# One rotation of PSUM banks, and small scalars moved off the vector engine, in a two-pass nucleus attention layer

## The chip, the cores and the metric

The kernel runs on one core of a Trainium2 chip. The metric is the device time of one execution in microseconds (us). The engines are TensorE (PE: matmuls and transposes, with its weight loads shown as PEld), VectorE (DVE), ScalarE (ACT), GpSimd (POOL) and SyncE (SP, which issues most transfers). Each takes its own instructions in order; semaphores tie them together.

## The reference

Two layers work on 4096 nodes of 256 features. Layer 0 is a graph attention with four heads over a 4096 x 4096 adjacency, plus a residual and a layer norm. Layer 1 does two steps. In each, every node gets a row of attention probabilities, cut to the smallest set whose mass reaches 0.9 (top-p), and its features are mixed with that row; a second stream is mixed by the normalised adjacency:

```
R = S + eye;  R = R / R.sum(-1)
for n in range(2):
    logits = (Xa @ W1.T @ W2.T) @ (Xa @ W3.T).T
    A = top_p(softmax(logits), 0.9);  A = A / A.sum(-1)
    Xf = R @ Xf
    Xa = A @ Xa
    Z = Z + Xf @ U1[n].T + Xa @ U2[n].T
out = layernorm(x + layernorm(x + Z) * g + b)
```

## The kernel before, in words

The first 950 us or so are layer 0 (`graph_attention`), which the change leaves alone. Layer 1 is `nucleus_layer`. It takes 32 tiles of 128 rows twice: a first pass (`place_first`, step 0) and a second one (`place_second`, step 1). A row tile of the class `RowTile` goes through these parts:

- the queries: a transpose of its features (L833, copied at L835), q1 (L918, copy L922), q (L926, copies L931 and L934);
- eight blocks of logits, 128 x 512 each, by `logits` (L950), copied from PSUM to SBUF by ACT in `logits_evict` (L961);
- the row maximum (`top`, L972; in the second pass over all 4096 columns), `spread` (L979) and `exp` (L990) on ACT, a handful of scalars;
- estimates of the threshold and moves towards it. In the second pass the estimates 1 and 2 use `estimate_half`: ACT runs over half of the row twice, once with Relu and once with Sign (L1064, L1067), and sums. `join` makes a mass of these sums (L1086, L1089 and L1096, on DVE) and takes its logarithm (L1079); `move` ends with the exponential L1134, which gives the new threshold t;
- `lift`, `final` (L1052 over 4096 columns, into w), then `tops` (32 maxima of eight, L965), `sort` (L1164, L1166), `edge` (L1173 to L1191, which ends with `fit`), `inside` and `cut` (L1224 on DVE, L1228 on POOL);
- the product with the features: eight blocks are transposed (L1240), copied to SBUF (L1249, or L1247 on DVE) and multiplied into `ap` (L1258), which is evicted at L1268.

Beside this a `Mix` multiplies a tile of the adjacency with the other stream (L1318, in two parts: a short and a long one), in eight chunks, into `rp`, copied at L1337 (`fx`). Each chunk's adjacency is loaded by SP. A finished mix of step 1 goes on to its output rows: four transposes (L833, copied at L835) and products (L1379) into `zp`; `out_sum` adds the residual `res` (L1405); `stats` takes mean and variance (L1390, L1392). `rsqrt_by_exp` gives the inverse deviation: logarithm and exponential on ACT (L64, L66), v, u and r1 on the engine that it is given (L68, L74, L75). `scale` makes `less` (L1400) and scales the row on ACT (L1401). This happens twice: `out_norm` (with gain and bias on POOL, L1411 to L1413) and, after `out_stats`, `out_store`, which also stores the row.

The order of work on PE, ACT, DVE and POOL is written out by hand. Every part is placed at a time in units of a tile, from the tables T1 and T2; `carry_out` sorts the parts by time and issues them, and each engine takes its share in that order. The order of SP's transfers is left to the scheduler of the framework.

[...] Here two (`ps_lg`) go to logits, three (`ps_tr`) to transposes, and three are single ones: `misc` (q1, q, zp), `ap` and `rp`. Each pool hands out its banks in turn.

Of the kernel before, what the change touches and what calls it, by code (L numbers as in the profile page):

```python
# [8 lines left out]
F32 = mybir.dt.float32  # L9
# [7 lines left out]
AF = mybir.ActivationFunctionType  # L17
# [5 lines left out]
P = 128  # L23
# [727 lines left out]
def nucleus_layer(  # L751
# [16 lines left out]
    ps_lg = ctx.enter_context(tc.tile_pool(name="f_lg", bufs=2, space=PSUM))  # L768
    ps_tr = ctx.enter_context(tc.tile_pool(name="f_tr", bufs=3, space=PSUM))
# [33 lines left out]
    shares = row("shares", SHARES)  # L803
    aims = [row(f"aims{n}", [aim for aim, _, _ in e]) for n, e in enumerate(EST)]
# [24 lines left out]
    def transposed(src, name, tag, bufs):  # L829

        tp = ps_tr.tile([P, 512], F32, tag="tr", name=f"tp_{name}")
        for c in range(2):
            nc.tensor.transpose(tp[:, c * P : (c + 1) * P], src[:, c * P : (c + 1) * P], ident)  # L833
        t = two.tile([P, 2, P], F32, tag=tag, name=f"t_{name}", bufs=bufs)
        nc.scalar.copy(t.rearrange("p c i -> p (c i)"), tp[:, : 2 * P])  # L835
        return t
# [38 lines left out]
    def keys(b):  # L875

        xt = []
        for c in range(2):
            tp = ps_tr.tile([P, 512], F32, tag="tr", name=f"tpk{b}_{c}")
            for q in range(4):  # L880
                nc.tensor.transpose(
                    tp[:, q * P : (q + 1) * P], xa[:, b * 4 + q, c * P : (c + 1) * P], ident
                )
            t = two.tile([P, 512], F32, tag="at", name=f"xkt{b}_{c}", bufs=3)
            if c:
                nc.scalar.copy(t, tp)
            else:
                nc.vector.tensor_copy(t, tp)
            xt.append(t)
        kp = ps_lg.tile([P, 512], F32, tag="lg", name=f"kp{b}")  # L890
# [8 lines left out]
    class RowTile:  # L899
# [12 lines left out]
        def front_transpose(self):  # L912
            self.xt = transposed(self.cur[:, self.i, :], f"x{self.id}", "xt", 3)

        def front_q1(self):
            qp = ps_one.tile([P, 512], F32, tag="misc", name=f"qp{self.id}")
            for c in range(2):
                nc.tensor.matmul(  # L918
                    qp[:DA, :P], w1[:, c, :], self.xt[:, c, :], start=c == 0, stop=c == 1
                )  # L920
            self.q1 = two.tile([DA, P], F32, tag="q1", name=f"q1_{self.id}", bufs=1)
            nc.scalar.copy(self.q1, qp[:DA, :P])  # L922

        def front_q(self):
# [3 lines left out]
            )  # L928
            self.q = two.tile([P, 2, P], F32R, tag="q", name=f"q_{self.id}")
            self.qp = qp[:, :P]  # L930
# [6 lines left out]
        def logits(self, pair):  # L937

            if pair == 0:
# [6 lines left out]
            self.lps[pair] = []  # L946
            for b in (2 * pair, 2 * pair + 1):
                lp = ps_lg.tile([P, 512], F32, tag="lg", name=f"lp{self.id}_{b}")
                for k in range(2):
                    nc.tensor.matmul(  # L950
                        lp,
                        self.q[:, k],
                        kT[:, b * 512 : (b + 1) * 512],
                        start=k == 0,
                        stop=k == 1,
                    )
                self.lps[pair].append((b, lp))

        def logits_evict(self, pair):
            for b, lp in self.lps.pop(pair):  # L960
                nc.scalar.copy(self.p[:, b * 512 : (b + 1) * 512], lp)  # L961

        def tops(self, src, b):
            for c in range(b * 4, (b + 1) * 4):
# [37 lines left out]
        def scalars(self):  # L1002
# [10 lines left out]
            self.aim = self.tiny("aim", len(self.est))  # L1013
# [3 lines left out]
        def scalars2(self):  # L1017
# [14 lines left out]
            else:  # L1032
                nc.vector.tensor_scalar(self.left, self.z, TOP_P - 1.0, None, ALU.mult)
                self.rest = small
                self.rzs = self.tiny("rzs", 2)
                nc.vector.tensor_scalar(self.rzs, shares, self.rz, None, ALU.mult)
# [45 lines left out]
        def join(self, k):  # L1082
            b, share = self.b, 0 if self.n and k == 0 else None
            if self.n and k:

                nc.vector.tensor_scalar(  # L1086
                    self.m, self.signs, self.t_half, self.t_all, ALU.mult, ALU.add
                )
                nc.vector.tensor_scalar(  # L1089
                    self.m, self.m, self.gaps, 0.0, ALU.subtract, ALU.max  # L1090
                )
# [4 lines left out]
                nc.vector.tensor_scalar(self.both, self.m, b, None, ALU.add)  # L1096
# [72 lines left out]
        def edge(self):  # L1169
# [13 lines left out]
            if self.n:  # L1183
# [6 lines left out]
                nc.vector.tensor_scalar(self.fit, out_of, -1.0, float(R), ALU.mult, ALU.add)  # L1190
                nc.vector.tensor_scalar(self.fit, self.fit, over, None, ALU.subtract)  # L1191
# [39 lines left out]
        def tops_of_pair(self, pair):  # L1231
            for b in (2 * pair, 2 * pair + 1):
                self.tops(self.p, b)

        def product_transpose(self, b):
            if b == 0:
                self.a_t = {}
            tp = ps_tr.tile([P, 512], F32, tag="tr", name=f"tpa{self.id}_{b}")
            for q in range(4):
# [4 lines left out]
                )  # L1244
            at = two.tile([P, 512], F32, tag="at", name=f"at{self.id}_{b}", bufs=3)
# [36 lines left out]
    class Mix:  # L1282
# [82 lines left out]
        def out_load_x(self):  # L1365
            rows = slice(self.i * P, (self.i + 1) * P)
            self.res = two.tile([P, D], F32, tag="res", name=f"res{self.id}", bufs=1)
            nc.sync.dma_start(self.res, x1_d[rows, :])

        def out_transpose(self, k):  # L1370
            src = xa[:, self.i, :D] if k == 2 else (self.xf1, self.fx[:, :D], None, self.xa2)[k]
            self.ot = transposed(src, f"o{k}{self.id}", "xt", 3)
# [14 lines left out]
        def stats(self, name):  # L1387
# [6 lines left out]
                nc, nc.vector, tiny, self.mv[:, 1:2], eps, f"{name}{self.id}"  # L1394
            )

        def scale(self):
            r = self.rstd()
            less = tiny.tile([P, 1], F32, tag="u", name=f"less{self.id}")
            nc.vector.tensor_scalar(less, self.mv[:, 0:1], r, -1.0, ALU.mult, ALU.mult)  # L1400
            nc.scalar.activation(self.h, self.h, AF.Identity, scale=r, bias=less)  # L1401

        def out_sum(self):
            self.h = two.tile([P, D], F32, tag="h", name=f"h{self.id}", bufs=1)
# [20 lines left out]
    def at(time, part, *args):  # L1425
# [7 lines left out]
        lag=0.218, out=0.344, qt=0.253, q1=0.460, q2=0.612, q3=0.680, space=0.125, apart=0.250, split=0.300,  # L1433
    )
    T2 = dict(top=0.468, spread0=0.650, spread1=0.516, exp0=0.655, exp1=0.607, scalars=0.731, scalars2=0.769, est0=0.808, join0=0.810, move0=0.828, join1=0.945, move1=1.088, est2=1.144, join2=1.232, move2=1.395, lift=1.491, final=1.649, tops=1.651, sort=1.842, edge=2.034, inside=2.135, cut=2.230, product=2.354, lag=0.090, out=0.060, qt=-0.086, q1=0.421, q2=0.453, q3=0.523, space=0.067, apart=0.074, mix=0.576, copy=0.042)
# [6 lines left out]
    def place_product(t, time, T):  # L1442
        space = T["space"]
        for k in range(8):
            at(time + k * space, t.product_transpose, k)
            at(min(time + k * space + T["lag"], time + 8 * space - 0.001), t.product, k)
# [3 lines left out]
    def place_queries(t, time, T):  # L1450
        at(time + T["qt"], t.front_transpose)
        at(time + T["q1"], t.front_q1)
        at(time + T["q2"], t.front_q)
        at(time + T["q3"], t.front_q_rest)

    def place_mix(m, time, length):

        for jc in range(8):
            at(time + (jc - 3.5) * length / 8, m.load, jc)
            at(time + jc * length / 8 + 0.03, m.mix, jc)  # L1460
# [4 lines left out]
    def place_first(t, time):  # L1465

        place_queries(t, time - 1, T1)
        for k in range(4):
            at(time + k * T1["apart"] + 0.01, t.logits, k)
            at(time + k * T1["apart"] + 0.01, t.logits_evict, k)  # L1470
            at(time + k * T1["apart"] + T1["tops"], t.tops_of_pair, k)
# [24 lines left out]
    def place_second(t, time):  # L1496

        place_queries(t, time - 1, T2)
        for k in range(4):
            at(time + k * T2["apart"] + 0.01, t.logits, k)  # L1500
            at(time + k * T2["apart"] + T2["copy"], t.logits_evict, k)
# [25 lines left out]
    def place_out(m, time):  # L1527
# [3 lines left out]
        for k in range(4):  # L1531
            at(time + 0.01 + 0.09 * k, m.out_transpose, k)
            at(time + 0.06 + 0.09 * k, m.out_product, k)
        at(time + 0.36, m.out_sum)
        at(time + 0.46, m.out_norm)
        at(time + 0.62, m.out_stats)
        at(time + 0.70, m.out_store)
# [457 lines left out]
```

## Time and profile before

| what | us |
|---|---|
| median of 3 runs (3446.21 to 3450.65) | 3448.2 |
| the profiled execution | 3446.17 |
| its span | 3444.2 |
| PE busy | 3120.7 |
| DVE busy | 2881.3 |
| ACT busy | 2528.7 |
| POOL busy | 611.2 |

The profile gives busy time by engine, in the whole span or in stretches of it; the granted clock of PE as a share of full speed; groups of instructions by line, with the mean time of one in ns; and waits, each put down to the instruction that ended it. Layer 0 takes up to about 950 us, the first pass from there to 1780, the second pass to 3380, and the last output rows run to the end. A wait on one engine costs nothing while another is the limit, so the stretches have to be read one by one.

### The profile page before, as it was taken

The page shows a single profiled execution, that of the slowest core. Times are in us where ns is not written, and L with a number is a line of the kernel's source. Part 1 is how long each engine was busy: PE and PEld are TensorE (multiplying, and loading weights), DVE is VectorE, ACT ScalarE, POOL GpSimd, SP SyncE. Part 2 cuts the span into 40 slices and gives each one's busy share as a digit, 9 for nine tenths or more (in the row PEclk, how much of TensorE's full clock was granted, in tenths as well). Part 3 has the DMA queues.
Part 4 walks back from the last instruction along what each step waited for, and adds up shares of the span by engine and source line. Part 5 has one row for each costly group of instructions (what it writes and reads, how often), then busy time and mean ns, then how long its engine had stood idle before and what let it go on. Part 6 is the DMA issues. An engine that isn't in the chain of part 4 may idle for free. (4 is left out here: it accounts for less than half of the span.)

```text
span 3444.2 us, 56052 instructions
## 1 busy us (share of the span) xinstructions
PE 3120.7 (91%) x19538; PEld 2162.0 (63%) x19538; DVE 2881.3 (84%) x8687; ACT 2528.7 (73%) x3978; POOL 611.2 (18%) x435
## 2 busy tenths in 40 slices
PE   8998888888889999999997898989899999999986
PEld 4422222222268888888875677777677777777775
DVE  4779989999848888888714999999999999899983
ACT  4678888888758888888725777777767667767752
POOL 1101450000000000000000222222222333343332
PEclk9999999999989999999998999999999999999998
DMA  9846453332152222322336444444644444444443
GB/s 214 138 114 138 131 131 113 114 111 86 62 167 95 96 105 107 108 95 95 103 100 172 116 116 126 119 118 126 169 111 113 109 112 110 110 111 116 112 104 78
DMA packets 637302, 402.60 MB, mean 117 GB/s; under 512 B 262672, under 2 KB 588304, under 8 KB 633936
## 3 DMA queue, kind: packets, MB, share of 16 engines
q1 hardware_dynamic: 626640, 315.03, 32.4%
q10 hardware_dynamic: 1536, 67.11, 5.4%
q0 software_dynamic: 8832, 16.78, 5.3%
q8 instruction: 155, 2.54, 0.3%
q14 instruction: 139, 1.14, 0.1%
HBM read 406.03 MB, written 118.62 MB: 152 GB/s over the span
## 5 line engine op out<-in xcount | busy, mean ns | idle before, releaser
L1318 PE MATMUL rp<-low,adj 128*128 128x258 f32 x1856 | 542.8, 382 | 26.7 <-ACT fx L1337 14.6
L1318 PE MATMUL rp<-p,short 128*128 128x256 f16 x1856 | 494.6, 293 | 2.2 <-DMA short<-adj_d 2.1
L1258 PE MATMUL ap<-xa,at 128*128 128x257 f32 x2048 | 490.9, 382 | 4.9 <-ACT at L1249 4.8
L617 DVE COPY_PREDICATED other<-mask,e 128x2048 f32<-128x2048 uint8 x176 | 454.0, 2594 | 49.3 <-ACT other L602 47.3
L1258 PE MATMUL ap<-xf,at 128*128 128x257 f32 x2048 | 483.5, 380 | 0.0
L950 PE MATMUL lp<-kT,q 128*128 128x512 f32 x1024 | 339.7, 458 | 106.0 <-ACT p L961 105.6
L595 ACT ACTIVATE e<-src,minus_flat,factors 128x2048 f32<-128x2048 f32 x176 | 367.9, 2090 | 71.3 <-DVE other L617 34.2
L1318 PEld LDWEIGHTS rp<-low,adj 128*128 128x128 f32 x1856 | 387.9, 209 | 49.3 <-ACT fx L1337 20.7
L647 PE MATMUL acc<-other,v 128*32 128x512 f32 x2816 | 345.4, 609 | 79.4 <-DVE other L617 67.0
L1258 PEld LDWEIGHTS ap<-xf,at 128*128 128x128 f32 x2048 | 381.1, 190 | 55.1 <-DVE at L1247 0.3
L1258 PEld LDWEIGHTS ap<-xa,at 128*128 128x128 f32 x2048 | 372.6, 191 | 54.2 <-ACT at L1249 6.7
L1249 ACT COPY at<-tpa 128x512 f32<-128x512 f32 x448 | 261.7, 585 | 153.1 <-PE tpa L1240 151.0
L602 ACT ACTIVATE other<-away,minus_flat 128x2048 f32<-128x2048 f32 x176 | 350.6, 1992 | 7.4 <-PE acc L647 6.2
L1228 POOL TENSOR_TENSOR p<-p,w 128x1024 f32<-128x1024 f32 x128 | 300.6, 2369 | 256.9 <-DVE w L1224 217.1
L1240 PE MATMUL tpa<-ident,p 128*128 128x128 f32 x2048 | 312.0, 276 | 2.6 <-POOL p L1228 2.6
L961 ACT COPY p<-lp 128x512 f32<-128x512 f32 x512 | 275.3, 583 | 46.3 <-PE lp L950 45.5
L950 PEld LDWEIGHTS lp<-kT,q 128*128 128x128 f32 x1024 | 193.6, 212 | 152.0 <-ACT p L961 119.2
L647 PEld LDWEIGHTS acc<-other,v 128*32 128x32 f32 x2816 | 80.8, 111 | 308.4 <-DVE other L617 158.1
L1240 PEld LDWEIGHTS tpa<-ident,p 128*128 128x128 f32 x2048 | 248.2, 142 | 39.5 <-POOL p L1228 3.2
L979 ACT ACTIVATE junk_s<-p,htop 128x2048 uint8<-128x2048 f32 x128 | 256.3, 2002 | 18.5 <-DVE htop L974 18.4
L1224 DVE MATCH_REPLACE8 w<-c,w 128x128 f32<-128x128 f32 x1024 | 268.0, 276 | 0.0
L990 ACT ACTIVATE p<-p,ntop 128x2048 f32<-128x2048 f32 x128 | 258.3, 2018 | 1.0
(271 smaller groups left out, 5483.3 us busy)
## 6 DMA issues: line engine op xcount, KB each, us to landing
adj<-adj_d SPq DMA_DIRECT2D x464, 256.0 KB
mask<-adj_d SPq DMA_DIRECT2D x164, 256.0 KB
short<-adj_d SPq DMA_DIRECT2D x232, 128.0 KB
mask<-mask_d SPq DMA_DIRECT2D x60, 256.0 KB
adj<-in_adjT SPq DMA_DIRECT2D x48, 256.0 KB
mask<-in_adjT POOLq DMA_DIRECT2D x32, 256.0 KB, 8.1
adj_d<-mask SPq DMA_DIRECT2D x32, 256.0 KB
src<-src_d SPq DMA_DIRECT2D x8, 1024.0 KB
```

Source lines behind the costliest of these rows:

```text
L595: nc.scalar.activation(self.e, self.head.src, AF.Relu, scale=self.factor(0), bias=self.factor(2))
L602: nc.scalar.activation(self.other, self.head.away, AF.Identity, bias=self.factor(2))
L617: nc.vector.copy_predicated(self.other, self.mask, self.e)
L647: nc.tensor.matmul(head.acc[k][at : at + 32, :], weights, self.e[:, b * 512 : (b + 1) * 512], tile_position=(0, at), **ends,)
L950: nc.tensor.matmul(lp, self.q[:, k], kT[:, b * 512 : (b + 1) * 512], start=k == 0, stop=k == 1,)
L961: nc.scalar.copy(self.p[:, b * 512 : (b + 1) * 512], lp)
L1224: nc.vector.match_replace(w[:, cols], self.cand[:, c * TOP : (c + 1) * TOP], w[:, cols], 0.0)
L1228: nc.gpsimd.tensor_tensor(self.p[:, cols], self.p[:, cols], w[:, cols], ALU.subtract)
L1240: nc.tensor.transpose(tp[:, q * P : (q + 1) * P], self.p[:, (b * 4 + q) * P : (b * 4 + q + 1) * P], ident,)
L1249: nc.scalar.copy(at, tp)
L1258: nc.tensor.matmul(self.ap[:, : D + 1], at[:, q * P : (q + 1) * P], self.cur[:, j, :], start=j == 0, stop=j == NT - 1,)
L1318: nc.tensor.matmul(self.rp[:, : part.shape[1]], a, part, start=start and k == 0, stop=stop and k == len(parts) - 1,)
```

## The change

It has four parts.

- The pools `ps_lg` and `ps_tr` become one pool of five banks that logits, keys and all transposes take in turn. Parts that used to make a PSUM tile and copy it at once are split in two (`front_copy`, `front_q1_copy`, `front_q_copy`, `out_copy`, `product_copy`), so that each half has a time of its own; logits are placed block by block.
- The layer norm's scalars of the output rows (v, u, r1, less) and `fit` go from DVE to GpSimd. The shares' scaling is folded into the one of the aims.
- In `join` the sums of the half estimates go from DVE to ScalarE: an Identity with scale and bias, a Relu, and an Identity for `both`.
- `h` and `res` get two buffers each, and T2 gets new times: among others the last move goes from 1.395 to 1.461, behind the copies of the queries; the output parts out_norm, out_stats and out_store go from 0.46, 0.62 and 0.70 to 0.54, 0.74 and 0.92 of a tile after the output's start; a mix's chunks start 0.072 of a tile after its start and lie closer together. T1 stays, but for the new keys.

```diff
-    ps_lg = ctx.enter_context(tc.tile_pool(name="f_lg", bufs=2, space=PSUM))
-    ps_tr = ctx.enter_context(tc.tile_pool(name="f_tr", bufs=3, space=PSUM))
+    ps = ctx.enter_context(tc.tile_pool(name="f_tr", bufs=5, space=PSUM))
...
-                self.rzs = self.tiny("rzs", 2)
-                nc.vector.tensor_scalar(self.rzs, shares, self.rz, None, ALU.mult)
+                self.rzs = self.aim[:, len(self.est) :]
...
-                nc.vector.tensor_scalar(
-                    self.m, self.signs, self.t_half, self.t_all, ALU.mult, ALU.add
-                )
-                nc.vector.tensor_scalar(
-                    self.m, self.m, self.gaps, 0.0, ALU.subtract, ALU.max
-                )
+                nc.scalar.activation(
+                    self.m, self.signs, AF.Identity, scale=self.t_half, bias=self.t_all
+                )
+                nc.scalar.activation(self.m, self.gaps, AF.Relu, scale=-1.0, bias=self.m)
...
-                nc.vector.tensor_scalar(self.both, self.m, b, None, ALU.add)
+                nc.scalar.activation(self.both, self.m, AF.Identity, bias=b)
...
-                nc.vector.tensor_scalar(self.fit, out_of, -1.0, float(R), ALU.mult, ALU.add)
-                nc.vector.tensor_scalar(self.fit, self.fit, over, None, ALU.subtract)
+                nc.gpsimd.tensor_scalar(self.fit, out_of, -1.0, float(R), ALU.mult, ALU.add)
+                nc.gpsimd.tensor_scalar(self.fit, self.fit, over, None, ALU.subtract)
...
-            self.res = two.tile([P, D], F32, tag="res", name=f"res{self.id}", bufs=1)
+            self.res = two.tile([P, D], F32, tag="res", name=f"res{self.id}", bufs=2)
...
-                nc, nc.vector, tiny, self.mv[:, 1:2], eps, f"{name}{self.id}"
+                nc, nc.gpsimd, tiny, self.mv[:, 1:2], eps, f"{name}{self.id}"
...
-            nc.vector.tensor_scalar(less, self.mv[:, 0:1], r, -1.0, ALU.mult, ALU.mult)
+            nc.gpsimd.tensor_scalar(less, self.mv[:, 0:1], r, -1.0, ALU.mult, ALU.mult)
...
-            self.h = two.tile([P, D], F32, tag="h", name=f"h{self.id}", bufs=1)
+            self.h = two.tile([P, D], F32, tag="h", name=f"h{self.id}", bufs=2)
...
-            at(time + jc * length / 8 + 0.03, m.mix, jc)
+            at(time + jc * (length - T2["gap"]) / 8 + T2["gap"], m.mix, jc)
...
-        for k in range(4):
-            at(time + k * T2["apart"] + 0.01, t.logits, k)
-            at(time + k * T2["apart"] + T2["copy"], t.logits_evict, k)
+        for k in range(8):
+            when = time + k // 2 * T2["apart"] + k % 2 * T2["block"]
+            at(when + 0.01, t.logits, k)
+            at(when + T2["copy"], t.logits_evict, k)
...
-            at(time + 0.06 + 0.09 * k, m.out_product, k)
+            at(time + 0.01 + 0.09 * k + T2["olate"], m.out_copy)
+            at(time + 0.07 + 0.09 * k, m.out_product, k)
         at(time + 0.36, m.out_sum)
-        at(time + 0.46, m.out_norm)
-        at(time + 0.62, m.out_stats)
-        at(time + 0.70, m.out_store)
+        at(time + 0.54, m.out_norm)
+        at(time + 0.74, m.out_stats)
+        at(time + 0.92, m.out_store)
```

The times of T2 that differ otherwise are: top 0.468 to 0.474, spread1 0.516 to 0.568, exp1 0.607 to 0.583, scalars 0.731 to 0.750, scalars2 0.769 to 0.774, est0 0.808 to 0.798, est2 1.144 to 1.179, lift 1.491 to 1.520, edge 2.034 to 1.977, cut 2.230 to 2.221, qt -0.086 to -0.048, q1 0.421 to 0.440, q2 0.453 to 0.457, q3 0.523 to 0.528, copy 0.042 to 0.045.

## The prediction

> **What bounds the kernel now.** I read the time by stretches first. After "us" the columns are busy time of PE, PEld, DVE, ACT and POOL, the granted clock, DMA share and GB/s. The three rows stand for the first pass, the second pass while it makes no output rows ("A", 1920 to 2540), and the second pass with them ("B", 2556 to 3320).
>
> ```profile
> 1300.00:1450.00 150.00, 150.00 (x795) 127.36 (x794) 131.45 (x482) 129.80 (x255) 5.14 (x12) 1.00 0.28 101
> 1920.00:2540.00 620.00, 555.27 (x3294) 451.65 (x3294) 583.14 (x2321) 462.56 (x845) 153.53 (x93) 0.94 0.50 127
> 2556.00:3320.00 764.00, 702.32 (x4172) 577.90 (x4170) 703.28 (x2830) 551.73 (x1115) 254.58 (x157) 0.96 0.45 112
> ```
>
> The first pass is PE alone: busy throughout, at full clock. In A, DVE is busy 94% and PE 90%; in B both 92%. So the waits decide there. Those of A (us in total, times, longest):
>
> ```profile
> PE lp L950 <- ACT p L961: 54.9, 17, 5.8
> DVE s L1125 <- ACT y L1079: 7.5, 14, 1.0
> DVE halves L1086 <- ACT halves L1071: 4.6, 6, 1.3
> ```
>
> And of B:
>
> ```profile
> PE lp L950 <- ACT p L961: 35.4, 13, 3.2
> DVE h L1405 <- PE zp L1379: 14.6, 15, 2.4
> PE qp L918 <- DVE h L1405: 10.7, 10, 2.7
> ACT h L1401 <- DVE less L1400: 12.8, 13, 2.2
> PE rp L1318 <- ACT fx L1337: 7.3, 8, 2.7
> ```
>
> PE's largest wait is for a logits bank: two banks, whose copies stand on ACT behind the two 2 us passes of a half estimate. Short stretches around one such wait show that it costs twice; the clock is the third number from the right, and the first row is the wait itself.
>
> ```profile
> 2343.50:2347.60 4.10, 0.22 (x2) 0.03 (x1) 4.10 (x18) 4.07 (x8) 0.00 (x0) 0.87 0.57 136
> 2347.60:2351.20 3.60, 3.56 (x13) 2.68 (x13) 3.53 (x26) 2.43 (x6) 2.63 (x2) 0.50 0.00 0
> 2351.20:2354.80 3.60, 3.60 (x20) 2.77 (x20) 3.60 (x29) 2.08 (x6) 3.60 (x2) 0.70 0.66 162
> 2354.80:2358.00 3.20, 3.20 (x27) 2.65 (x26) 2.91 (x9) 1.69 (x4) 3.20 (x3) 1.00 0.72 167
> ```
>
> PE idles 4 us, then runs 7 us at 0.5 and 0.7. DVE stays full, so in A this wait delays nobody: A is DVE's, B is shared.
>
> A tile takes 43.8 us in A (thirteen row maxima from 1917.30 to 2486.13) and 50.6 in B (fifteen, 2528.73 to 3287.61): 14.2 and 15.1 tiles. B makes 27 outputs, two scalings each.
>
> **The small sums leave DVE.** Their rows over the second pass:
>
> ```profile
> L1086 DVE TENSOR_SCALAR halves<-halves 128x1 f32<-128x1 f32 x64 | 17.0, 265 | 15.0 <-ACT halves L1071 14.7
> L1089 DVE TENSOR_SCALAR halves<-halves 128x1 f32<-128x1 f32 x64 | 13.7, 214 | 2.3
> L1070 ACT ACTIVATE halves<-t 128x1 f32<-128x1 f32 x64 | 11.9, 186 | 0.0
> L74 DVE TENSOR_SCALAR ua<-r0a,va 128x1 f32<-128x1 f32 x32 | 8.5, 265 | 1.7 <-ACT r0a L66 1.2
> L1400 DVE TENSOR_SCALAR less<-mva,r1a 128x1 f32<-128x1 f32 x32 | 6.9, 214 | 1.1
> ```
>
> Per tile go two of L1086 (0.265) and two of L1089 (0.214), one of L1096 (0.214), both fits of L1190 and L1191 (0.149, 0.214) and the shares of L1036 (0.219): 1.75 us, and eight gaps of 0.036 (2.3/64): 2.03 us. Per scaling go L68 (0.154), L74, L75 (0.214) and L1400: 0.85, with gaps 0.99. In A that is 14.2 x 2.03 = 29 us; in B 15.1 x 2.03 + 54 x 0.99 = 84 us.
>
> Here a rule speaks against the change: the Trainium skill, "VectorE: DVE Perf Modes", section "The TRN2 errata", gives DVE a fixed 58 cycles at 0.96 GHz (0.06 us) and ScalarE 224 at 1.2 GHz (0.19 us). By it the moves save DVE only 0.8 us a tile and 0.4 a scaling with gaps (A 11, B 34). The rows decide: 0.15 to 0.27 us on DVE, 0.186 on ACT. ACT gains five such, 0.9 us a tile; it is busy 75% of A and 72% of B, and the sums now follow their inputs on the same engine.
>
> On POOL no tensor_scalar is in the trace. Nearest is the 128x1 copy of L1272, 0.18 us, so u, r1 and less take about 0.65 with gaps, against 0.80 on DVE. "GPSIMD Engine Reference", section 4.1, calls GpSimd some 2x slower for two inputs and near line rate for one: 1.6 by that. Both ends are hidden: in one B tile the exponent was ready at 2932.52 and the scaling ran at 2937.75. What would uncover them is a lock, which the trace does show:
>
> ```profile
> 2937.82 4.48 DVE L1052 SCALAR_TENSOR_TENSOR w<-p,tf 128x4096 f32<-128x4096 f32 x1
> 2938.42 4.48 POOL L1411 TENSOR_TENSOR h<-h,gb 128x256 f32<-128x256 f32 x1 [7.46 <-ACT h L1401]
> 2942.86 0.73 POOL L1412 TENSOR_TENSOR res<-res,gb 128x256 f32<-128x256 f32 x1
> 2400.80 4.41 DVE L972 TENSOR_REDUCE ntop<-p 128x1 f32<-128x4096 f32 x1
> 2401.90 0.68 POOL L852 TENSOR_TENSOR sc<-sc,hi 128x256 f32<-128x256 f32 x1
> ```
>
> A 0.73 us POOL operation started under the long DVE operation of two inputs lasts until that ends; under the row maximum it doesn't. In the new order the sums of an output come just ahead of the row maximum, so most scalars fall under it: free.
>
> **One rotation of five banks.** A bank's next owner is five allocations later, whatever its kind. In the first pass PE's order stays (but for the last tiles' mixes). The tight pairs there: a logits bank was empty by 1308.24 and its successor started at 1309.54 or later; the eighth transposed block, copied by DVE, was done at 1317.34 and its bank is next wanted at 1321.45. Cost 0; a late copy there would cost PE its length.
>
> In the second pass the third logits pair no longer needs the first pair's copies after the half estimate. From the first logits of a B tile PE has 10.9 us of work before it needs something behind that estimate: four logits 2.1, two transposes 0.8, an output product 1.0, three mix chunks 6, and two more logits 1.0. ACT reaches it after two copies, an output copy, a scaling, the move and the estimate (two passes of 2.2 with their readouts), two more copies and a t_o copy: about 11.3. So the wait falls from 2.3 us a tile (35.4/15.1) to about 0.4. The mixes' later start (gap 0.072) takes PE's 7.3 us wait for fx away.
>
> Sum for PE in B: waits 60 us (all its rows), of which 29 of the logits' and 7 of fx's go; its busy 702 us at clock 0.96 would lose up to 28 at full clock, and I take half, since half of the waits stay. 764 - 36 - 14 = 714. DVE's own floor is 764 - 84 = 680 with its waits kept, so PE sets B: **50 us saved** (bounds: 0 if the stall only moves; 88 with all waits and clock loss gone). In A PE would be far below (620 - 65 - 33), so DVE sets it: **29 saved** (up to 46, with its 17 us of waits gone). The start of the second pass (1780 to 1920) holds 13.5 us of the logits wait, partly under DVE's: 5 saved (0 to 13).
>
> **Stages moved and waits added.** The last move's exponential now stands on ACT behind the copies of the queries and an output's second scaling; the lift on DVE waits for it, and the long final pass behind that. In the B tile above the cast of q ended at 2935.62; 0.60 for the scaling and 0.30 for t make 2936.5, when the row maximum ends (2936.47): 0 to 0.2 us for 27 outputs, 3 us. In A the cast ended at 2360.39 and the maximum at 2361.18: nothing. The first scaling of every second output waits on POOL behind fit, so behind the edge on DVE; up to 0.7 us for 13 outputs, ahead of t and the half estimate: 3 us. The stores are issued by SP 0.22 of a tile later, and an adjacency load behind one waits with it; but a load waits for the mix three chunks earlier anyway, and the mix waited only 0.5 us for adjacency in B: 0. The second h and res buffers are what lets a store at 0.92 overlap the next sum at 0.86; no wait row for them exists: 0. In the tail two more handovers to POOL: 1 us.
>
> Sum: 29 + 50 + 5 - 3 - 3 - 1 = 77. The profiled execution took 3446.2 (a span of 3444.2 and 2 around it), which gives 3369; the median of the runs, 3448.2, is 2 us above it, so **3371**.
>
> **Rivals.** *Both floors.* With DVE's waits in A and PE's clock in B recovered: 46 + 88 + 10 = 144, so 3304. For it: the stalls and their slow clocks feed each other. Against: h<-zp, qp<-h and s<-y are true dependences, which stay.
>
> *The stall moves.* ACT is 2 us later than I count, and transposes and output products now wait in the one rotation as logits did. B saves about 20, the sum is 29 + 20 + 5 - 7 = 47: 3401. For it: 11.3 against 10.9 is tight.
>
> *POOL locks ACT (slower).* If the scalars meet the final pass, as h<-h,gb did in 14 of 27 cases at about 4.4 us, ACT stands before the scaling, and behind it t, which DVE waits for. It decides where it eats the gain of 84 us over 54 scalings, at 1.6 us each reaching DVE; at 2.5 us it is 135 - 84 = 51 slower: 3499. Against: the order puts them under the row maximum, and ACT has 212 us idle in B.
>
> **How the numbers follow.** Main case 0.52 (3340 to 3395), both floors 0.16, moved stall 0.18, lock 0.12, nothing 0.02. About 0.2% is what a measurement here can tell from no change. Faster 0.86, same 0.02, slower 0.12. Range 3308 to 3420: from near the first rival's time past the second's, the third's left out.
>
> **What would show it.** Right: the logits wait under 10 us in A and B, clock at 0.98 or more, DVE busy per tile down by 2 (A) and 5.5 us (B), tiles of some 41.7 and 47 us. Wrong: long waits of ACT h for POOL, of DVE's lift for t, or of PE's transposes or output products for ACT.

## The result, and the profile after

The changed kernel takes 3390.7 us (median of four runs, 3380.5 to 3396.1) against 3447.2 for the kernel before beside it: a ratio of 0.9836, 95% interval 0.9818 to 0.9853. It is faster, by 57 us at the medians and by 65.7 between the two profiled executions (3446.17 and 3380.48). I had said 3371.

To see where the time went I cut the second pass at the starts of the row maximum on DVE, one a tile: "A" is the third to the seventeenth (14 tiles without output rows), "B" from there to the last (15 tiles with them).

| profiled execution | before, us | after, us | gained | forecast |
|---|---|---|---|---|
| up to the first row maximum | 1832.4 | 1824.2 | 8.1 | 0, and 5 for the first tiles of the second pass |
| the first two tiles | 84.9 | 85.9 | -1.0 | in the 5 |
| A (a tile: 43.67, after 42.06) | 611.4 | 588.8 | 22.6 | 29 |
| B (a tile: 50.59, after 48.60) | 758.9 | 729.0 | 29.9 | 50 |
| after the last row maximum | 156.6 | 150.6 | 6.0 | -1 |

The first row maximum lay between 1822 and 1836 in the 13 profiles of this study and the last stretch took 150 to 163 us, so the 8.1 and the 6.0 can't be told apart from what profiles differ by. A and B are the change: 52.5 of the 57 us by the medians. They come from one profile of each kernel, and the runs of the kernel after lie 16 us apart, so a difference of 2 to 4 us in a stretch says little by itself.

The stretches, with the columns of the first fence of the prediction: A and B of the kernel before at these cuts, then a piece of the first pass, A and B of the kernel after.

```profile
1917.30:2528.73 611.43, 547.80 (x3246) 444.99 (x3245) 574.67 (x2307) 456.30 (x835) 153.49 (x94) 0.94 0.50 128
2528.73:3287.61 758.88, 697.70 (x4141) 574.54 (x4141) 698.25 (x2810) 547.54 (x1106) 252.17 (x154) 0.96 0.44 112
...
1300.00:1450.00 150.00, 150.00 (x796) 127.08 (x795) 131.89 (x481) 132.00 (x261) 6.00 (x14) 1.00 0.26 94
1910.10:2498.91 588.81, 536.16 (x3228) 433.93 (x3227) 555.53 (x2194) 471.37 (x902) 162.39 (x122) 0.97 0.52 132
2498.91:3227.92 729.01, 683.35 (x4149) 567.00 (x4147) 637.81 (x2483) 564.71 (x1179) 305.47 (x389) 0.98 0.46 116
```

The first pass is as before, PE without a gap. In A, DVE's busy time fell from 574.7 to 555.5 us and is still 94% of the stretch. In B it fell from 698.3 to 637.8 (87%); PE is busy 94%. The clock rose from 0.94 to 0.97 and from 0.96 to 0.98.

The waits of the kernel after in A (us in total, times, longest):

```profile
PE lp L961 <- ACT p L966: 29.8, 12, 5.9
PE ap L1261 <- ACT at L1252: 10.3, 14, 1.9
```

And in B:

```profile
PE zp L1385 <- ACT t_o L837: 31.3, 12, 3.7
PE rp L1321 <- ACT fx L1340: 5.3, 4, 2.5
PE lp L961 <- ACT p L966: 1.8, 1, 1.8
DVE h L1411 <- PE zp L1385: 42.7, 23, 5.1
```

The logits wait of B is gone (35.4 before, 1.8 now). In its place PE waits 31.3 us for the copy of an output's transpose, in 12 of the 15 tiles, and behind that product DVE's output sum waits for `zp`: 42.7 us, 15.3 before. PE's wait for the output sum (`qp` for `h`, 10.7 before) is gone too. In A half of the logits wait is left.

One such place in the timeline of the kernel after: start, duration, engine, line, operation. PE first, from the tile's first logits to the product that waits; then ACT.

```profile
2575.11 1.18 PE L961 MATMUL lp<-kT,q 128*128 128x512 f32 x4
2577.25 1.17 PE L961 MATMUL lp<-kT,q 128*128 128x512 f32 x4
2580.24 1.17 PE L961 MATMUL lp<-kT,q 128*128 128x512 f32 x4
2581.25 0.28 PE L1321 MATMUL rp<-low,adj 128*128 128x258 f32 x1
2582.11 0.28 PE L1321 MATMUL rp<-p,short 128*128 128x256 f16 x1
2584.58 1.13 PE L1385 MATMUL zp<-u,t_o 128*128 128x256 f32 x4 [2.20 <-ACT t_o L837]
...
2578.91 1.99 ACT L1069 ACTIVATE junk_s<-p,t 128x2048 uint8<-128x2048 f32 x1
2581.02 2.00 ACT L1072 ACTIVATE junk_s<-p,t 128x2048 uint8<-128x2048 f32 x1
2583.21 1.04 ACT L966 COPY p<-lp 128x512 f32<-128x512 f32 x2
2584.16 0.38 ACT L837 COPY t_o<-tp_o 128x256 f32<-128x256 f32 x1
```

The last two rows before the wait are the first and the last product of a mix chunk. PE has its work done at 2582.38; the copy that it needs stands on ACT behind the two passes of the half estimate and a pair of logits copies, and ends at 2584.54.

### The profile page after: what moved, and what is told of

The parts are those of the page before. It is cut to its first block, busy times and chain, and to the rows that moved or that the text cites. A ratio compares the mean times of both kernels' runs of the same rounds, so it can differ in the third digit from the quotient of the medians.

```text
span 3378.5 us, 55965 instructions
## 1 busy us (share of the span) xinstructions
PE 3081.9 (91%) x19538; PEld 2138.2 (63%) x19538; DVE 2786.4 (82%) x8175; ACT 2570.3 (76%) x4138; POOL 655.9 (19%) x755
## 5 line engine op out<-in xcount | busy, mean ns | idle before, releaser
L1321 PE MATMUL rp<-low,adj 128*128 128x258 f32 x1856 | 540.3, 381 | 33.8 <-ACT fx L1340 19.6
L1261 PE MATMUL ap<-xa,at 128*128 128x257 f32 x2048 | 492.4, 383 | 13.3 <-ACT at L1252 13.1
L617 DVE COPY_PREDICATED other<-mask,e 128x2048 f32<-128x2048 uint8 x176 | 452.6, 2584 | 45.6 <-ACT other L602 45.1
L961 PE MATMUL lp<-kT,q 128*128 128x512 f32 x1024 | 316.4, 430 | 44.3 <-ACT p L966 35.3
L1321 PEld LDWEIGHTS <-short 128*128 128x128 fp8e4 x1856 | 182.4, 98 | 108.8 <-issue 14.9
```

Source lines behind the costliest of these rows:

```text
L617: nc.vector.copy_predicated(self.other, self.mask, self.e)
L961: nc.tensor.matmul(lp, self.q[:, k], kT[:, b * 512 : (b + 1) * 512], start=k == 0, stop=k == 1)
L1261: nc.tensor.matmul(self.ap[:, : D + 1], at[:, q * P : (q + 1) * P], self.cur[:, j, :], start=j == 0, stop=j == NT - 1,)
L1321: nc.tensor.matmul(self.rp[:, : part.shape[1]], a, part, start=start and k == 0, stop=stop and k == len(parts) - 1,)
```

## The experiments

Two theories. *Mine by then*: two engines hold the second pass in turn, so that neither DVE's relief nor the banks pay alone, and what the banks free is stopped again by the next thing that PE needs from behind the half estimate on ACT. *The rival*, which is the prediction's arithmetic: in A each us taken from DVE counts, in B PE's waits count, and each part of the change brings its own share. A second question is which moved scalars matter.

All times of the runs, with A and B of their profiles. The runs were made beside runs of the kernel before in four groups, with medians of that kernel of 3447.2, 3445.1, 3442.0 and 3442.1 us; so kernels of different groups are compared by their ratios.

| kernel | median, us | ratio to before | 95% interval | A | B |
|---|---|---|---|---|---|
| before | 3447.2 | 1 | | 611.4 | 758.9 |
| after | 3390.7 | 0.9836 | 0.9818 to 0.9853 | 588.8 | 729.0 |
| the moved scalars alone | 3448.4 | 1.0001 | 0.9989 to 1.0013 | 609.1 | 757.6 |
| the rotation alone | 3438.9 | 0.9993 | 0.9983 to 1.0003 | 607.5 | 757.7 |
| after, old times | 3413.1 | 0.9905 | 0.9888 to 0.9923 | 592.8 | 742.9 |
| after, nothing moved off DVE | 3431.2 | 0.9964 | 0.9947 to 0.9982 | 604.7 | 748.6 |
| after, two pools | 3456.3 | 1.0035 | 1.0022 to 1.0049 | 630.3 | 753.7 |
| after, layer norm's scalars on DVE | 3397.5 | 0.9854 | 0.9829 to 0.9880 | 590.3 | 741.0 |
| after, sums on DVE | 3403.2 | 0.9886 | 0.9868 to 0.9903 | 601.4 | 730.9 |
| after, Sign pass later | 3363.1 | 0.9748 | 0.9723 to 0.9773 | 592.1 | 699.9 |
| after, whole half estimate later | 3367.5 | 0.9787 | 0.9770 to 0.9804 | 590.2 | 706.6 |
| before, Sign pass later | 3456.1 | 1.0035 | 1.0021 to 1.0049 | 610.3 | 767.2 |
| Sign pass later, slope on GpSimd in A | 3346.7 | 0.9720 | 0.9704 to 0.9737 | 585.2 | 698.7 |

### The parts alone and left out

**The moved scalars alone.** The kernel before with the half estimates' sums on ACT and the layer norm's scalars and fit on GpSimd; pools, times and shares as before.

```diff
-                nc.vector.tensor_scalar(
-                    self.m, self.signs, self.t_half, self.t_all, ALU.mult, ALU.add
-                )
+                nc.scalar.activation(
+                    self.m, self.signs, AF.Identity, scale=self.t_half, bias=self.t_all
+                )
...
-                nc, nc.vector, tiny, self.mv[:, 1:2], eps, f"{name}{self.id}"
+                nc, nc.gpsimd, tiny, self.mv[:, 1:2], eps, f"{name}{self.id}"
```

> The kernel before with only the moves off DVE: layer norm's scalars and fit on GpSimd, the half estimates' sums on ScalarE. Two pools, the old times and single buffers stay. If DVE was the limit in the stretch without outputs and PE's stalls in the other, the first gains its 1.6 us a tile (25 us) and the second some 10 to 15: 3405 to 3415. If DVE's load was all that mattered, the two gain 29 and 84: about 3335.

Both missed: 1.0001. The stretches of A and B in this run, with the columns of before:

```profile
1922.50:2531.64 609.14, 542.08 (x3227) 439.77 (x3226) 557.60 (x2209) 477.24 (x905) 159.58 (x122) 0.95 0.50 128
2531.64:3289.28 757.64, 699.92 (x4162) 574.97 (x4161) 635.73 (x2498) 571.05 (x1181) 318.36 (x392) 0.97 0.45 113
```

And of its waits two of A and, last, one of B:

```profile
PE lp L950 <- ACT p L961: 58.5, 22, 5.9
DVE rs L1272 <- ACT ax L1266: 13.0, 11, 3.3
...
DVE rank L1205 <- POOL fit L1189: 29.9, 12, 2.6
```

DVE is busy 17 us less in A and 62.5 less in B, and the stretches are 2 and 1 us shorter. In A the logits wait stays at 58.5 us, and DVE, no longer full, now waits where it hardly did before (rs for ax 13.0, before 0.9). PE's busy time and its waits, 542 and 67 us, fill the 609 of the stretch. So in A the logits wait was not free: it held the same length of tile from PE's side. In B 29.9 us of the relief go into a wait for fit.

**The rotation alone.** The kernel before with one pool of five banks and nothing else.

```diff
-    ps_lg = ctx.enter_context(tc.tile_pool(name="f_lg", bufs=2, space=PSUM))
-    ps_tr = ctx.enter_context(tc.tile_pool(name="f_tr", bufs=3, space=PSUM))
+    ps_tr = ctx.enter_context(tc.tile_pool(name="f_tr", bufs=5, space=PSUM))
...
-                lp = ps_lg.tile([P, 512], F32, tag="lg", name=f"lp{self.id}_{b}")
+                lp = ps_tr.tile([P, 512], F32, tag="tr", name=f"lp{self.id}_{b}")
```

> The kernel before with one pool of five banks for logits, keys and transposes, and nothing else: the times, the copies right behind their products and the scalars on DVE as before. Theory (rotation and new times pay only together, since the order of the copies on ACT decides what stands behind the half estimate): little by itself, 3425 to 3450. Rival (the five banks alone are the gain, the rest is decoration): 3385 to 3400, with the logits wait of B near 2 us.

0.9993, as my theory said. The waits of A (the first two) and of B:

```profile
PE lp L949 <- ACT p L960: 21.1, 11, 5.6
PE qq L925 <- ACT q L921: 19.7, 13, 2.8
...
PE zp L1378 <- ACT t_o L834: 22.0, 11, 2.6
PE qp L917 <- DVE h L1404: 17.0, 11, 3.4
```

In A the logits wait fell from 54.9 to 21.1 and A by 4 us. PE's waits did not get fewer, they moved: 68 us in all, 63 before. DVE is as busy as before (573.65 of 607.46), which fits DVE as the limit there. In B the logits wait is off the list, and B is as long as before: PE waits for the output's copy (22.0, not on the list before) and for the output sum (17.0, before 10.7). Every kernel here with one rotation has this wait for the copy in B (7.8 us or more); of the four with two pools none has more than 1.3 us of it.

**Both, with the old times.** All places of T2, the mixes' and the outputs' go back (move2 to 1.395, edge to 2.034, and so on). The second buffers of `h` and `res` and the folded shares stay, which neither of the two runs before had.

```diff
-        at(time + 0.54, m.out_norm)
-        at(time + 0.74, m.out_stats)
-        at(time + 0.92, m.out_store)
+        at(time + 0.46, m.out_norm)
+        at(time + 0.62, m.out_stats)
+        at(time + 0.70, m.out_store)
```

> The changed kernel with all times of the kernel before (the stages where they were, each copy right behind its product); the rotation, the moved scalars and the second buffers stay. Theory (new times are needed): 3415 to 3445, with waits of DVE for y and for fit as in the run of the moves alone. Rival (times are a trifle beside the rotation and the moves): 3385 to 3400.

0.9905: 2 us below my range and 13 above the rival's. Two parts that bring nothing alone bring 0.95% together (A 18.6 us, B 16.0). What the second buffers have in it was not run by itself; A makes no output rows, so its 18.6 are not theirs, and the folded shares can have 3 of them at most (14 tiles of 0.22). The rest comes with the times: A 4.0, B 13.9. Which of them matter was not taken apart. One of the waits that they take away is DVE's for fit in B, in this run:

```profile
DVE rank L1210 <- POOL fit L1194: 29.8, 12, 2.6
```

In the timeline fit stands on POOL behind the three operations of an output's gain and bias: in one tile these take from 2536.37 to 2539.1, the two operations of fit follow, and DVE goes on at 2539.66, after a wait of 2.60 us. The wait is not on the list of the changed kernel, where `edge` with fit stands 0.057 of a tile (2.8 us) earlier and `out_norm` 0.08 later, so that fit goes ahead of these three.

**Nothing moved off DVE**, with rotation and new times: all sums, layer norm scalars, fit and shares back on DVE.

> The changed kernel with everything that left DVE put back there (the half estimates' sums, the layer norm's scalars, fit, the shares); the rotation, the new times and the second buffers stay. Theory (DVE's load does not set the time, the stalls do): 3397 to 3410, DVE busy back by some 90 us and the time by 7 to 20. Rival (DVE is the floor in A and near it in B, as the prediction had it: 29 in A and the part of B above the PE floor come back): 3430 to 3455.

0.9964, in the rival's range: 1.3% of the 1.6% is lost (44 us of 3447), not 7 to 20. A of this run:

```profile
1915.84:2520.52 604.68, 539.69 (x3238) 435.56 (x3236) 572.99 (x2306) 450.86 (x832) 156.54 (x94) 0.96 0.51 130
```

DVE's busy time is 17.5 us higher in A than in the changed kernel and A is 15.9 longer: one to one, nearly. In B it is 65 higher, and B 19.6 longer. My theory that DVE's load doesn't matter falls for A: with the rotation there it does.

**Two pools**, with moved scalars and new times: `kp` and `lp` back in two banks of their own, three for transposes.

```diff
-    ps = ctx.enter_context(tc.tile_pool(name="f_tr", bufs=5, space=PSUM))
+    ps = ctx.enter_context(tc.tile_pool(name="f_tr", bufs=3, space=PSUM))
+    ps_lg = ctx.enter_context(tc.tile_pool(name="f_lg", bufs=2, space=PSUM))
```

> The changed kernel with logits and keys in two banks of their own and the transposes in three, as before the change; all else stays. If the rotation is what took the logits wait away, that wait comes back: some 50 us of PE in the stretch without outputs, where DVE is the limit and it costs little, and 30 us or more with outputs, where PE and DVE share it. Time about 3410 to 3420. If the rotation only moved the stall to the output products, nothing is lost: 3385 to 3395.

Both missed by 36 us or more: 1.0035, slower than before and 2.0% above the changed kernel. The waits of A (the first two) and of B:

```profile
PE lp L962 <- ACT p L967: 61.7, 22, 5.9
DVE f L1148 <- ACT t L1138: 16.0, 5, 7.5
...
PE lp L962 <- ACT p L967: 46.5, 18, 4.4
DVE h L1412 <- PE zp L1386: 62.7, 23, 5.2
```

The logits wait of A is back above where it was before (54.9), and the last move, placed behind the copies of the queries, makes DVE's lift wait for t: 16.0 us, up to 7.5 in one place. That is the coupling that the prediction priced at 3 us for B and at nothing for A. The changed kernel shows no wait of the lift for t: with these times, the rotation keeps it at nothing.

### Which scalars

**Layer norm's scalars back on DVE**, and **the sums back on DVE**, each in the changed kernel.

```diff
-                nc, nc.gpsimd, tiny, self.mv[:, 1:2], eps, f"{name}{self.id}"
+                nc, nc.vector, tiny, self.mv[:, 1:2], eps, f"{name}{self.id}"
...
-            nc.gpsimd.tensor_scalar(less, self.mv[:, 0:1], r, -1.0, ALU.mult, ALU.mult)
+            nc.vector.tensor_scalar(less, self.mv[:, 0:1], r, -1.0, ALU.mult, ALU.mult)
```

> The changed kernel with the layer norm's scalars v, u, r1 and less back on DVE (fit stays on GpSimd). It gives DVE 54 x 0.99 = 53 us back in the stretch with outputs. If PE's waits behind the half estimate set that stretch, DVE has room (busy 638 of 729 us) and about 15 to 25 are lost: 3405 to 3415. If DVE sets it, all 53 are lost: about 3444.

```diff
-                nc.scalar.activation(self.m, self.gaps, AF.Relu, scale=-1.0, bias=self.m)
+                nc.vector.tensor_scalar(
+                    self.m, self.m, self.gaps, 0.0, ALU.subtract, ALU.max
+                )
...
-                nc.scalar.activation(self.both, self.m, AF.Identity, bias=b)
+                nc.vector.tensor_scalar(self.both, self.m, b, None, ALU.add)
```

> The changed kernel with the sums of the half estimates (Identity, Relu and the Identity for both, on ACT) back on DVE, as in the kernel before; all else of the change stays, fit and the layer norm's scalars on GpSimd too. Theory (putting all the moved scalars back cost 40 us, putting the layer norm's back 7; so the rest sits in these sums, which DVE pays most often: five a tile, 1.2 us): 3410 to 3422, A back up by 10 to 14 us. Rival (the rest sits in fit and the shares, or only all together count): 3391 to 3402.

Putting the layer norm's scalars back costs 0.2% (0.9854 against 0.9836), and the intervals overlap, so that the times alone do not tell it from nothing; by the profiles it is 12 us in B. Either way it is less than either theory had. The sums are worth 0.5%, some 17 us, of which the profiles show 12.6 in A. That is the place that I had named; the time, 3403.2, falls between the two ranges. In A the sums bring nearly all that is lost with all scalars back (12.6 of 15.9). In B some 6 of the 19.6 are left for fit, the shares and what only shows when all are together.

### What stops B

**The Sign pass later**, in the changed kernel: the half estimate's Relu stays in its place, and the Sign pass with what follows it goes, for the last estimate, behind the copies of the second logits pair and of an output's transpose.

```diff
+        def estimate_half_signs(self):
+            cols = self.p[:, N // 2 :]
             nc.scalar.activation(
                 junk_s, cols, AF.Sign, bias=self.t, scale=-1.0, accum_out=self.signs
             )
...
                 at(time + T2[f"move{k - 1}"] + 0.002, t.estimate_half)
+                at(time + (0.0, 0.8345, 1.150)[k], t.estimate_half_signs)
```

> The changed kernel with the half estimate's two passes on ScalarE placed apart: Relu at its old place, then the copies of a logits pair and of an output transpose, then Sign. If the second output product waits because its transposed block is copied behind both passes, PE's wait of 31 us in the stretch with outputs falls under 10, DVE's wait for zp falls with it, and about 1 to 2 us a tile are gained: 3360 to 3378. If other dependences set the stretch, the time stays within 5 us of 3390.

3363.1, a ratio of 0.9748: 0.9% below the changed kernel (0.9748 / 0.9836), all of it in B. The stretches A and B of this run:

```profile
1914.47:2506.55 592.08, 537.70 (x3228) 435.94 (x3226) 555.75 (x2195) 470.77 (x903) 162.43 (x122) 0.96 0.52 132
2506.55:3206.50 699.95, 679.00 (x4140) 561.97 (x4140) 637.45 (x2482) 561.13 (x1179) 306.86 (x389) 0.99 0.48 121
```

And of its waits two of A and, last, one of B:

```profile
PE tpa L1242 <- POOL p L1234: 23.0, 11, 3.5
PE lp L961 <- ACT p L966: 4.9, 5, 3.5
...
PE zp L1388 <- ACT t_o L837: 8.0, 13, 1.4
```

The output product's wait falls from 31.3 to 8.0 us and B by 29.1. PE is now busy 97% of B. In A the logits wait falls too, from 29.8 to 4.9, and A is not shorter: PE waits 23.0 for the cut in its place, while DVE's busy time is the same (555.75).

**The whole half estimate later.** Both passes at 1.150, not cut in two.

```diff
-                at(time + T2[f"move{k - 1}"] + 0.002, t.estimate_half)
+                at(time + (T2["move0"] + 0.002, 1.150)[k - 1], t.estimate_half)
```

> The changed kernel with the last half estimate placed later as a whole: both passes at 1.150 of a tile, behind the copies of two logits pairs and of an output's transpose, not split. Theory (what counts is which copies stand behind the passes, not that they are cut in two): 3355 to 3375, like the split one, with the wait of the output product for its copy in B under 15 us. Rival (4.4 us of passes stall PE wherever they stand; only the cut helps): 3380 to 3400, with the wait now at the next logits pair or at a mix.

3367.5, inside the first range: most of the gain (B 706.6) needs no cut, only that the copies which PE needs first stand ahead. The product's wait in B is over the 15 us that I had given it:

```profile
PE zp L1385 <- ACT t_o L837: 18.6, 21, 2.1
```

**The Sign pass later in the kernel before.** The same edit, with two pools and the old times.

> The kernel before, with the second of the half estimate's two passes (Sign) placed later on ACT, behind the copies of the second logits pair (at 1.150 of a tile for the last estimate); nothing else. Theory (what PE stands behind is the pair of passes on ACT in a row; its place, and not the number of banks, is the lever): the logits wait of 90 us in A and B falls by half and the time to 3405 to 3430. Rival (with two banks the stall just moves to the next pair, behind the Sign pass): 3440 to 3455.

1.0035, slower: the rival's side, if just over its range. The waits of A (the first), and of B:

```profile
PE lp L950 <- ACT p L961: 35.9, 28, 3.5
...
PE qp L918 <- DVE h L1408: 43.6, 14, 4.4
PE lp L950 <- ACT p L961: 15.6, 24, 3.7
```

The logits wait falls from 90 to 52 us in A and B, about the half that I expected, and nothing comes of it: A is DVE's, and in B PE waits for the output sum instead (43.6, before 10.7). Why that sum is so late here was not followed further. So the order on ACT alone is no lever in this kernel. What makes it one in the changed kernel, the banks, the new times or DVE's lighter load, was not separated: the moved scalars alone had brought that same wait for the sum from 10.7 to 2.5 us.

### How far A is DVE's

The kernel with the Sign pass later, and in A the last four of the seven scalars of the last move's slope on GpSimd. All seven are also placed earlier there, at 1.319 and 1.320 of a tile.

```diff
+            e = nc.gpsimd if self.i < 15 else nc.vector
+            less, square, more, error = self.part
+            e.tensor_scalar(more, self.moved, less, square, ALU.mult, ALU.mult)
...
+        at(time + (1.319 if t.i < 15 else T2["move2"] - 0.001), t.slope_first)
+        at(time + (1.320 if t.i < 15 else T2["move2"] - 0.0005), t.slope)
```

> The split kernel (the changed kernel with the Sign pass later), and in the tiles of A also the last four of the seven scalars that make the last move's slope on GpSimd in place of DVE (1.1 us a tile on DVE), ahead of the last part of the cut there. Theory (with one rotation, A is DVE's and each us taken from it counts): A shorter by 10 to 15 us, 3348 to 3353. Rival (A is by now held by PE's waits for the cut and for copies): A within 4 us of 592, 3359 to 3367; with the cut's last part 1.5 us later it may even be slower.

0.9720, the lowest of all ratios, though its interval overlaps with that of the Sign pass alone. A's stretch:

```profile
1916.13:2501.35 585.22, 536.08 (x3239) 435.75 (x3239) 542.69 (x2143) 470.92 (x906) 182.27 (x179) 0.97 0.52 134
```

And two of DVE's waits in it:

```profile
DVE rs L1291 <- ACT ax L1285: 8.6, 10, 1.8
DVE all_z L1010 <- ACT p L996: 5.2, 5, 2.4
```

DVE is busy 13.1 us less and A is 6.9 us shorter, between the two theories. By this one pair of profiles half of the us count by now, and DVE's waits for ACT take some of the others (ax 8.6, before this edit 6.6; p 5.2, before 0.6). The median, 3346.7, is a little under my range all the same; the profiled execution was the slowest of four, 3352.3.

## Why the prediction was right, and where it was not

**The sign and the order of size** were right, and 3390.7 lies between the main forecast and the moved stall (3401), about halfway. The sum of 77 was 57 at the medians and 65.7 between the profiled executions, with 22.6 and 29.9 in A and B instead of 29 and 50. Of the 65.7, 13 lie outside A and B, where 4 had been forecast and where profiles differ by as much.

**"PE sets B: 50 saved": the wait left behind the half estimate was mis-sized, and the timeline shows by which term.** The step reckoned PE's work from the first logits to what it needs from behind the half estimate at 10.9 us, and ACT's at 11.3, so that 0.4 us of waiting were left. In the fence above PE has the work of just that list (six logits blocks, two transposes, an output product, three mix chunks) and runs dry after 7.27 us (2575.11 to 2582.38); ACT is through after 9.43 (to 2584.54): 2.2 us here, and 1.9 to 3.7 in 12 of 15 tiles. The three chunks had been put at 6 us. A chunk takes 1.0 to 1.2 us (1.13 in the fence), and did so in the trace of before too: four pairs of products from 2926.98 to 2928.15. So PE's side was 3.6 us too long, 2.9 of them in the chunks, and ACT's 1.9 us; the difference, put at 0.4, is 2.2. PE's waits in B, over all its rows, fell from 61 to 45 us in place of the 36 less that were forecast; the recovered clock, taken at half of 28, was right: PE's busy time fell by 14.3. 16 and 14 make the 30. Even the 16 had luck in it: the wait of `qp` for the output sum, which the prediction called a dependence that stays, went away with 10.7 us. The logits' wait gave 34 and fx 2, and the new wait took 31.

**The rival "the stall moves" is what happened in B, on the row that it named**: the output product. Its reasons were not: ACT was not later than counted but 1.9 us earlier, and what the product waits for is the copy of its own input, not a bank. Moving the passes later, whole or cut, takes 13 or 23 us from that wait and shortens B by 22 or 29 us at nearly equal busy times of all engines (PE's falls by 8 or 4). B is then 52 or 59 us shorter than before: the 50 that the step had expected and missed. That shows that this wait is what kept B from it.

**"In A DVE sets it: 29 saved"** stood with two faults. First, the size: the removed rows add up to 24.6 us in A (14 tiles) and 70.4 in B (26 outputs), and I added gaps to that; DVE's busy time fell by 19.1 and 60.4. Neighbouring small operations overlap in the record (a 0.15 us one at 2300.09, the next at 2300.16, in the kernel with the Sign pass later), so that their mean times add up to more than they occupy, and adding gaps makes it worse. The fixed 58 cycles of the Trainium skill ("VectorE: DVE Perf Modes", section "The TRN2 errata") had given 11 and 34, too little: the measured relief lies between the two, nearer to the rows. The prediction took that table row without the remark under it: the same section says that the row is too low for a single operation and that the fixed term measured about 150 cycles. That is 0.16 us, as the rows here have it for constants alone (0.15), and without gaps it gives an estimate of 18 and 52. Second, "this wait delays nobody": relieving the wait alone (54.9 to 21.1) gives 4 us in A, taking DVE's work alone 2, both with the old times 18.6. Each was the limit as soon as the other was relieved. The sum was right to put A down to DVE only because the rotation was in it.

**The moves' prices.** The rows of the moved scalars in the changed kernel, over its second pass:

```profile
L1091 ACT ACTIVATE halves<-halves 128x1 f32<-128x1 f32 x64 | 24.9, 390 | 0.0
L1094 ACT ACTIVATE halves<-halves 128x1 f32<-128x1 f32 x64 | 18.9, 295 | 2.1
L1099 ACT ACTIVATE halves<-halves,b 128x1 f32<-128x1 f32 x32 | 8.9, 279 | 0.0
L74 POOL TENSOR_SCALAR ua<-r0a,va 128x1 f32<-128x1 f32 x32 | 12.0, 374 | 2.3 <-ACT r0a L66 2.3
L75 POOL TENSOR_SCALAR r1a<-ua,r0a 128x1 f32<-128x1 f32 x32 | 11.3, 352 | 3.3
L1406 POOL TENSOR_SCALAR less<-mva,r1a 128x1 f32<-128x1 f32 x32 | 10.5, 329 | 3.2
```

ACT's sums take 0.28 to 0.39 us each, not 0.186: 1.65 us a tile, not 0.9. No harm of it shows: with the sums back on DVE, PE's waits in B are 43.7 us, against 45.1. On POOL u, r1 and less take 1.06 us in the first scaling and 0.89 in the second: above the 0.65 worked out from the copy's row, below 1.6, the estimate made from the Trainium skill ("GPSIMD Engine Reference", section 4.1) by counting them as operations of two inputs.

**"POOL locks ACT"** did not come. ACT's scaling waited for less 0.2 us in B, where it had waited 12.8 for DVE's before; in the whole second pass with its end it is 16.9 (11 times, 4.2 at most), nearly all behind the last row maximum. The lock itself is still there. The operation that now sits under DVE's long one of two inputs in 11 of the 26 outputs of B is `res` (L1418, 2.8 us against 0.73 free), which no engine waits for in B.

**The added waits** (3 for the lift, 3 for the scaling behind fit, 1 in the tail) were not seen where they were looked for: no wait of the lift for t in A or B, and 0.2 us of the scaling for POOL in B. (DVE's estimate waits 2.6 us for its t in B, which was on no list.) The first one is small because the rotation holds; with two pools it was 16 us in A. That the new times would matter by themselves (A 4.0, B 13.9, from the run with the old ones) was in the sum only as the mixes' 7 us. Of these, 2 came in B: PE's wait for fx is 5.3.

**What would show it**, by the numbers given: the clock 0.98 was met in B (0.97 in A); the logits wait under 10 us in B (1.8), not in A (29.8); DVE's busy time down 1.4 and 4.0 us a tile, not 2 and 5.5; tiles of 42.06 and 48.60, not 41.7 and 47. The row of PE's output product for ACT, named as a sign of error, is the one that appeared.

## What to carry to other kernels

Where two engines are both about 90% busy or more, do not price a relief or a freed wait alone: here two parts of the change gave 0.0 and 0.1%, and 0.95% together. Before a freed bank is booked as gain, walk down the waiting engine's queue to the next thing that comes from behind the same long operation, and time both queues with rows of the same trace: the difference of two sums needs each term right to its own size. In the changed kernel it was then enough to place the long operation behind the copies that others wait for.

## Not expected of the hardware

Not every wait of PE cost clock. Stretches of the changed kernel, the wait first and then what follows it; the granted clock is the third number from the right.

```profile
2582.38:2584.58 2.20, 0.01 (x1) 0.00 (x0) 2.20 (x19) 2.20 (x8) 1.36 (x2) 1.00 0.29 73
2584.58:2588.00 3.42, 3.42 (x20) 2.91 (x21) 3.39 (x25) 2.85 (x9) 3.42 (x2) 1.00 0.49 111
...
2970.12:2973.32 3.20, 0.00 (x2) 0.00 (x1) 3.20 (x25) 3.20 (x8) 2.27 (x3) 0.97 0.18 52
2973.32:2976.50 3.18, 3.18 (x11) 2.52 (x11) 3.15 (x23) 1.56 (x4) 3.18 (x2) 0.50 0.28 78
2976.50:2980.00 3.50, 3.50 (x23) 2.90 (x23) 2.48 (x19) 2.62 (x9) 3.33 (x4) 1.00 0.50 113
```

After 2.20 us of waiting PE went on at full clock, after 3.20 it had half of it for some 3 us. A wait of 5.85 us, in A, was followed by 0.50 and 0.54 for 8 us. Length alone does not decide: after a wait of 2.27 us, from 2235.95 to 2238.22, the next 3.3 us had 0.66, though the first product still took its full-speed 0.73 us.

The traces show what decides. In each of the 13 profiles the recorded clock changes only on a grid of 3.413 us; all 1032 changes lie within 0.002 us of it, and only its start differs between profiles. In A and B 4779 steps of this grid ran at full clock. The next step was at half clock after none of the 4429 in which PE idled less than 1.5 us, after 32 of the 132 with 1.5 to 1.9 us, and after 217 of the 218 with more. The wait of 2.27 us lies in one step, which ends at 2239.25; there the clock fell, 1 us after PE had gone on. Of the wait of 2.20 us, 1.62 lie before a boundary at 2584.00 and 0.58 behind it.

So part of a stall's price is a matter of its length and of where it falls. By these counts a lone wait of less than 1.5 us costs no clock; one of 3.8 us or more always does, as an estimate, since one step then holds at least 1.9 of it. Cutting a wait of 4 us to 2 can be worth more than 2.
